# Layer 0 of a two-layer transformer kernel: a PSUM bank of its own for the transposed mixed values, four score banks instead of five

## The chip, the cores and the metric

The kernel runs on one core of one Trainium2 chip. The metric is the device time of one execution in microseconds (us). Three runs of the kernel before gave 1212.03, 1212.92 and 1213.0 us; their median, 1212.92 us, is the time that the change is measured against.

## The reference, cut to what matters

The network is two pre-norm layers over x of 4 sequences x 512 tokens x 256 channels: attention, a routed feed-forward, a second attention, a gated feed-forward, each added to x. The change lies in the first attention (16 heads of 16 channels, causal, 512 tokens):

```python
qkv = jnp.einsum('bsd,od->bso', layernorm(x), w_project)      # q, k, v: 16 heads of 16
att = jnp.einsum('bhqd,bhkd->bhqk', q, k) / math.sqrt(16)
att = jnp.where(causal, -1e9, att)
att = softmax(att)
out = jnp.einsum('bhqk,bhkd->bhqd', att, v)                   # the mixed values
x = x + jnp.einsum('bsd,od->bso', out, w_out)
```

The routed feed-forward that follows in the same layer (router logits for 8 experts per output channel, the two best weighted, 8 expert products) is computed in the kernel at the same time as this attention, in pieces.

## The kernel before, in words

**Blocks and batches.** The 512 positions are cut into four blocks j of 128; block j attends to the keys of blocks 0 to j. A batch n is a block, one of the four sequences s, and a few of the four head groups g (four heads each): 4, 2, 1, 1 groups for j = 0, 1, 2, 3, so 4 + 8 + 16 + 16 = 44 batches (L595 to L600). A batch is treated in five steps:

- `greatest(n)` (L606): the scores with queries as rows, four matmuls per group (one per head, on four row tiles of 32 of TensorE), each head into a PSUM tile of its own of one bank (tag `sc`, L610).
- `mask(n)` (L621): adds the causal mask by matmuls with an identity, then DVE takes the row maxima, one reduction per head (L634).
- `shift(n)` (L639): transposes the maxima on TensorE into the pool `l0_mm` (tag `mm`, one bank), and DVE subtracts them from a row of the queries (L650).
- `powers(n)` (L654): the scores again, with keys as rows, into four more `sc` tiles (L658, matmuls at L664, head the innermost loop); ScalarE takes the exponentials, one instruction per head (L673); GpSimd zeroes the masked corner (L683).
- `mixed(n)` (L691): the product with the values, into the one bank of `l0_mm`, copied out to SBUF by ScalarE (L708).

When the four head groups of a block and sequence are done, `divided(j, s)` (L712) follows in pieces: four transposes of the mixed values into the tile `av_T` (L716, L718); DVE reads its column of sums, L724, and divides, L725, which ends the life of `av_T`; two more transposes `oq_T` (L731, L733), copied out at L736; after the fourth sequence the output products `o` (L742, L745), added to x by DVE (L754).

**Order.** The loop at L776 emits, for each n: `greatest(n+1)`, `shift(n)`, `mask(n+1)`, a `fill`, `mixed(n-1)`, `powers(n)`, another `fill`. A `fill` (L112) gives out work of the streams (generators) as long as a budget for TensorE and DVE lasts: the normalisation and projections of the next block (`prepare`, L561: tiles `x_ps`, `qk_ps`, `v_ps`), `divided`, and the feed-forward (`xT_ps`, `fold`, `lg_ps`, `eo`). The budgets and conditions count slots and made pieces, not PSUM. The instructions of TensorE, DVE and GpSimd keep this program order (`manual_schedule`, L63); in this layer the order of ScalarE and of the DMA queues is left to the framework, which also puts in all waits and gives each tile a bank of its pool when one is free.

**PSUM.** The eight banks: pool `dn`, two (L93; its tiles are `x_ps`, `qk_ps`, `v_ps`, `av_T`, `oq_T`, `o`, `xT_ps`, `fold`, `lg_ps`, `eo`, and it lives through the whole kernel); pool `l0_sc`, five (L437); pool `l0_mm`, one (L438). The last two are given back after layer 0, and the second attention takes those six banks.

The functions that the change touches:

Of the kernel before, what the change touches and what calls it, by code (L numbers as in the profile page):

```python
# [8 lines left out]
F32 = mybir.dt.float32  # L9
# [5 lines left out]
PSUM = bass.MemoryType.PSUM  # L15

P = 128
# [7 lines left out]
NH0 = 16  # L25
# [7 lines left out]
def tile_transformer(  # L33
# [62 lines left out]
    dn = ctx.enter_context(ExitStack())  # L96
    ps_dn = dn.enter_context(tc.tile_pool(name="dn", bufs=2, space=PSUM))
# [13 lines left out]
    def need(engine, cost, gap=0, cond=None):  # L111
        return engine, cost, gap, cond  # L112
# [143 lines left out]
    def hidden_pieces(b):  # L256

        out = []
        done = (4 * b - 5, 1)
        last = b == NBLK - 1  # L260
        yield from norm_pieces(b, b1, b2, out, cond=lambda: b < 2 or done in halves)
        xT = b2.tile([P, 2, 512], F32, tag="xT", name=f"xT{b}")
        for hc in range(2):
            yield need("PE", 0.5, 0 if hc else 1 + last)
            ps = transposed(out[0], hc, ps_dn, "dn", f"xT_ps{b}_{hc}")
            ps = ps.rearrange("p t q -> p (t q)")
            if hc:
                nc.scalar.activation(xT[:, hc, :], ps, AF.Identity, bias=last_16)
            else:
                nc.scalar.copy(xT[:, hc, :], ps)  # L270
        normed.clear()
        xTs[b] = xT
# [159 lines left out]
    with ExitStack() as l0:  # L432
# [1 line left out]
        a1 = l0.enter_context(tc.tile_pool(name="l0_1", bufs=1))  # L434
        a2 = l0.enter_context(tc.tile_pool(name="l0_2", bufs=2))
        a3 = l0.enter_context(tc.tile_pool(name="l0_3", bufs=3))
        ps_sc = l0.enter_context(tc.tile_pool(name="l0_sc", bufs=5, space=PSUM))  # L437
        ps_mm = l0.enter_context(tc.tile_pool(name="l0_mm", bufs=1, space=PSUM))  # L438

        wp = w0.tile([P, 2, 768], F32, name="wp")  # L440
        for hc in range(2):
# [270 lines left out]
        def divided(j, s):  # L712

            yield need("PE", 0.5, 1)
            avs = avs_of.pop((j, s))
            ps = ps_dn.tile([P, NH0, 32], F32, tag="dn", name=f"av_T{j}_{s}")  # L716
            for g in range(4):
                nc.tensor.transpose(  # L718
                    ps[:, 4 * g : 4 * g + 4].rearrange("p h d -> p (h d)"), avs[:, g], ident
                )  # L720
            rden = a2.tile([P, NH0], F32, tag="rden", name=f"rden_{j}_{s}")
            oq = a1.tile([P, NH0, 16], F32, tag="oq", name=f"oq_{j}_{s}")
            yield need("DVE", 0.7, 1)
            nc.vector.reciprocal(rden, ps[:, :, 16])  # L724
            nc.vector.tensor_tensor(  # L725
                oq, ps[:, :, 0:16], rden.unsqueeze(2).to_broadcast([P, NH0, 16]), ALU.mult
            )
            yield need("PE", 0.3, 1)
            if not s:
                aTs[j] = a1.tile([P, 2, 16, NS, 8], F32, tag="aT", name=f"aT{j}")  # L730
            ps = ps_dn.tile([P, 2, P], F32, tag="dn", name=f"oq_T{j}_{s}")  # L731
            for k in range(2):
                nc.tensor.transpose(  # L733
                    ps[:, k], oq[:, 8 * k : 8 * k + 8].rearrange("p h d -> p (h d)"), ident
                )
            nc.scalar.copy(aTs[j][:, :, :, s, :], ps.rearrange("p k (g b) -> p k g b", b=8))  # L736
            if s < NS - 1:
                return

            for t in (0, 2):  # L740
                yield need("PE", 1.75, 1)
                ps = ps_dn.tile([P, 2, HID], F32, tag="dn", name=f"o0_{j}_{t}")  # L742
                for i in range(2):
                    for k in range(2):
                        nc.tensor.matmul(  # L745
                            ps[:, i],
                            lhsT=aTs[j][:, k, 4 * (t + i) : 4 * (t + i) + 4].rearrange(
                                "p g s b -> p (g s b)"
                            ),
                            rhs=wo[:, k, :], start=k == 0, stop=k == 1,  # L750
                        )
                yield need("DVE", 0.7, 1)
                both = xres[:, 4 * j + t : 4 * j + t + 2, :]
                nc.vector.tensor_tensor(both, both, ps, ALU.add)  # L754
            fold_at = streams.index(fold) if fold in streams else len(streams) - 4
            streams.insert(fold_at, Stream(hidden_pieces(j)))


        ps = ps_mm.tile([P, 4, P], F32, tag="mm", name="idle")
# [16 lines left out]
        for n in range(NBT):  # L776
            j, s, gs = batches[n]
# [18 lines left out]
            if n and batches[n - 1][2][-1] == 3:  # L796
                streams.insert(0, Stream(divided(*batches[n - 1][:2])))
# [10 lines left out]
        mixed(NBT - 1)  # L808
        streams.insert(0, Stream(norm_pieces(0, b1, b2, normed_first)))
        last = Stream(divided(*batches[NBT - 1][:2]))  # L810
        streams.insert(0, last)
        while last.next is not None:
# [54 lines left out]
    with ExitStack() as l1:  # L867
# [199 lines left out]
        for p in range(-1, NP):  # L1067
            j, kv = divmod(p, NKV)
# [186 lines left out]
```

## Time and profile before

| | |
|---|---|
| three runs, us | 1212.03, 1212.92, 1213.0 |
| the profiled execution, us | 1213.42 |
| its span in the trace, first to last instruction, us | 1211.7 |
| TensorE busy (PE) | 1168.9 us, 7278 instructions |
| DVE busy | 802.6 us, 1780 instructions |
| ScalarE busy (ACT) | 485.5 us, 1101 instructions |
| layer 0 in the trace | up to about 426 us |
| `av_T`: transposes, reciprocals, divisions | 64, 16, 16 |
| score tiles in `l0_sc` | 176 of `greatest`, 176 of `powers` |

The profile is of one execution. The busy times are the sums of the recorded instructions of an engine; a matmul that has been handed to TensorE and still waits for a bank counts as busy in part, so a busy PE is not PE at work. In the lists, `out<-in` are the program's tile names, `xN` the number of instructions, and a bracket at the end of a line is the idle time of that engine before it and who ended it. PEld is the weight load of TensorE, which overlaps the matmuls.

### The profile page before, as it was taken

How to read it: one execution, taken by the hardware profiler on the slowest of the kernel's cores; microseconds unless marked ns; L12 is line 12 of the kernel's file. 1: busy time of each engine (PE TensorE's matmuls, PEld its weight loads, DVE VectorE, ACT ScalarE, POOL GpSimd, SP SyncE). 2: the span in 40 equal slices, each digit the busy share in tenths (PEclk: the TensorE clock that was granted, in tenths of full speed). 3: DMA queues.
4: the chain of work that ended last, by engine and by line, in shares of the span. 5: the costliest groups of instructions: out<-in, count | busy, mean ns of one | idle time of the engine just before them, and what ended most of it. 6: DMA issues, size and time to landing. Idle time of an engine off the chain costs nothing.

```text
span 1211.7 us, 18780 instructions
## 1 busy us (share of the span) xinstructions
PE 1168.9 (96%) x7278; PEld 679.8 (56%) x7278; DVE 802.6 (66%) x1780; ACT 485.5 (40%) x1101; POOL 121.1 (10%) x155
## 2 busy tenths in 40 slices
PE   6979999999999898999999999999999999999998
PEld 3656555555555543555555555656645456475487
DVE  2555589898887848737886395798499853735710
ACT  1233455664555444434444345355344321312300
POOL 8333321121111000000000000000000000000000
PEclk9899999999999998999999999999999999999999
DMA  7122102000000040000000001021020000000000
GB/s 221 17 56 54 19 4 34 2 1 1 2 1 2 27 147 1 1 1 1 1 1 1 1 1 36 10 55 43 1 62 9 1 1 17 1 1 18 0 1 35
DMA packets 21305, 26.78 MB, mean 22 GB/s; under 512 B 5120, under 2 KB 14592, under 8 KB 21216
## 3 DMA queue, kind: packets, MB, share of 16 engines
q1 hardware_dynamic: 20544, 24.40, 7.6%
q10 hardware_dynamic: 672, 1.18, 0.4%
q8 instruction: 57, 0.93, 0.3%
q14 instruction: 32, 0.26, 0.1%
HBM read 19.27 MB, written 2.10 MB: 18 GB/s over the span
## 4 chain that ended last, share of the span: by engine, by line
PE 81%; DVE 12%; ACT 2%; DMA 2%; issue 1%; SPq 1%; POOL 0%; ACTq 0%; DVEq 0%; POOLq 0%
PE qk_ps L928 10%; PE o L1019 9%; PE y L1175 9%; PE g L856 8%; PE u L856 8%; PE eo L226 8%; PE lg_ps L226 7%; PE s L614 4%; DVE mx L634 3%; PE s L664 3%; PE av L700 2%; PE v_ps L910 2%; PE qk_ps L529 2%; PE s L941 1%; PE a L999 1%
## 5 line engine op out<-in xcount | busy, mean ns | idle before, releaser
L928 PE MATMUL qk_ps<-xT,wqkv 128*128 128x512 f32 x320 | 148.7, 599 | 0.6 <-ACT qT L932 0.6
L226 PE MATMUL lg_ps<-rw,xT 128*128 128x512 f32 x256 | 123.8, 607 | 3.7 <-ACT xT L895 1.7
L226 PE MATMUL eo<-ew,xT 128*128 128x512 f32 x256 | 122.0, 600 | 1.3 <-ACT part L315 1.0
L1019 PE MATMUL o<-wpj,oT 128*128 128x256 f32 x512 | 119.8, 382 | 0.0
L634 DVE TENSOR_REDUCE mx<-s 128x1 f32<-128x384 f32 (+3 forms) x176 | 100.5, 634 | 20.3 <-PE s L629 20.3
L1175 PE MATMUL y<-wd,it 128*128 128x256 f32 x512 | 111.8, 379 | 0.0
L1019 PEld LDWEIGHTS o<-wpj,oT 128*128 128x128 f32 x512 | 95.9, 190 | 28.1 <-issue 15.1
L1175 PEld LDWEIGHTS y<-wd,it 128*128 128x128 f32 x512 | 97.1, 190 | 14.9 <-issue 2.2
L928 PEld LDWEIGHTS qk_ps<-xT,wqkv 128*128 128x128 f32 x320 | 59.3, 190 | 70.0 <-issue 60.2
L673 ACT ACTIVATE pt<-s 128x512 f32<-128x512 f32 (+1 forms) x176 | 83.7, 561 | 34.4 <-PE s L664 34.3
L856 PE MATMUL g<-xT,wgu 128*128 128x512 f32 x192 | 90.4, 593 | 0.0
L856 PE MATMUL u<-xT,wgu 128*128 128x512 f32 x192 | 90.2, 592 | 0.0
L315 ACT ACTIVATE part<-eo,c 128x256 f32<-128x256 f32 x128 | 53.7, 473 | 81.5 <-PE eo L226 76.9
L683 POOL TENSOR_SCALAR_AFFINE_SELECT pt<-pt 128x256 f32<-128x256 f32 (+2 forms) x88 | 55.2, 632 | 268.6 <-ACT pt L673 268.1
L1153 ACT ACTIVATE th<-sq 128x512 f32<-128x512 f32 x64 | 40.3, 629 | 87.6 <-DVE sq L1152 87.6
L177 POOL TENSOR_TENSOR ln_rs<-rs_v,minus_half 128x4 f32<-128x4 f32 x16 | 18.0, 1127 | 563.3 <-DVE rs_v L176 457.9
L226 PEld LDWEIGHTS lg_ps<-rw,xT 128*128 128x128 f32 x256 | 46.5, 192 | 49.0 <-issue 36.9
L226 PEld LDWEIGHTS eo<-ew,xT 128*128 128x128 f32 x256 | 46.4, 190 | 45.8 <-issue 37.0
L614 PE MATMUL s<-qk 32*128 32x128 f32 (+3 forms) x512 | 69.7, 478 | 1.3 <-DMA qk<-stage 0.5
L214 DVE TENSOR_TENSOR xres<-xres,y 128x256 f32<-128x256 f32 x16 | 6.7, 421 | 92.2 <-PE y L1175 92.2
L650 DVE TENSOR_TENSOR qk<-qk,mxT 128x128 f32<-128x128 f32 (+2 forms) x44 | 15.2, 346 | 77.0 <-PE mxT L645 69.3
L289 ACT COPY lg<-lg_ps 128x512 f32<-128x512 f32 x64 | 37.6, 587 | 64.5 <-PE lg_ps L226 64.3
(233 smaller groups left out, 1831.2 us busy)
## 6 DMA issues: line engine op xcount, KB each, us to landing
qk<-stage SPq DMA_DIRECT2D x56, 64.0 KB, 2.4
wqkv<-in_w_qkv SPq DMA_DIRECT2D x8, 320.0 KB, 6.0
rw<-in_router_w SPq DMA_DIRECT2D x8, 256.0 KB, 4.8
ew<-in_expert_w SPq DMA_DIRECT2D x8, 256.0 KB, 5.0
wpj<-in_w_proj SPq DMA_DIRECT2D x1, 2048.0 KB, 11.9
out<-xres SPq DMA_DIRECT2D x4, 512.0 KB, 2.6
xres<-in_x SPq DMA_DIRECT2D x3, 512.0 KB, 8.1
dq_wgu<-in_gate_w SPq DMA_DIRECT2D x8, 128.0 KB, 2.4
```

The costliest lines, as they stand in the source:

```text
L226: nc.tensor.matmul(ps, lhsT=xT[:, hc, (g % 4) * P : (g % 4 + 1) * P], rhs=w[:, hc, 2 * pair : 2 * pair + 2, :].rearrange("p e o -> p (e o) ...
L289: nc.scalar.copy(lg[:, 2 * pair : 2 * pair + 2, :].rearrange("p e o -> p (e o)"), ps)
L315: nc.scalar.mul(part[:, e % 4], ps[:, i], c[:, e : e + 1])
L614: nc.tensor.matmul(tiles[h][:, b * nk : (b + 1) * nk].rearrange("p (c k) -> p c k", k=P), lhsT=queries(j, g)[r, s], rhs=qk[r, g, : j + 1, ...
L634: nc.vector.tensor_reduce(maxes[n % 2][:, :nb, h, 0], ps[:, : nb * nk].rearrange("p (b k) -> p b k", b=nb), AX.X, ALU.max,)
L673: nc.scalar.activation(pt[:, i, : nb * nk], tiles[2 * pair + i][:, : nb * nk], AF.Exp, scale=0.25)
L683: nc.gpsimd.affine_select(out=last, in_=last, compare_op=ALU.is_ge, fill=0.0, base=0, pattern=pattern, channel_multiplier=-1,)
L856: nc.tensor.matmul(ps, lhsT=wgu[:, w, half, jj, par * P : (par + 1) * P], rhs=xT[:, half, :], start=half == 0, stop=half == 1,)
L928: nc.tensor.matmul(ps, lhsT=wqkv[:, hc, kv, h, :], rhs=xT[:, hc, :], start=hc == 0, stop=hc == 1,)
L1019: nc.tensor.matmul(ys[t // 2][:, t % 2], lhsT=state["o"][:, h, t * P : (t + 1) * P], rhs=wpj[:, HPK * kv + h, :], start=kv == 0 and h == 0 ...
L1153: nc.scalar.activation(th, sq, AF.Tanh, scale=0.7978845608028654)
L1175: nc.tensor.matmul(ps, lhsT=it[:, c // 2, c % 2, t * P : (t + 1) * P], rhs=wd[:, c // 2, c % 2, :], start=c == 0, stop=c == 2 * NJ - 1,)
```

## The change

The scores get four banks in place of five, and a new pool of one bank, `l0_t`, holds `av_T`, which was a tile of `dn`. Nothing else is changed: the number of banks, the instructions and the program order of TensorE, DVE and GpSimd stay as they are.

```diff
-        ps_sc = l0.enter_context(tc.tile_pool(name="l0_sc", bufs=5, space=PSUM))
+        ps_sc = l0.enter_context(tc.tile_pool(name="l0_sc", bufs=4, space=PSUM))
         ps_mm = l0.enter_context(tc.tile_pool(name="l0_mm", bufs=1, space=PSUM))
+        ps_t = l0.enter_context(tc.tile_pool(name="l0_t", bufs=1, space=PSUM))
...
             yield need("PE", 0.5, 1)
             avs = avs_of.pop((j, s))
-            ps = ps_dn.tile([P, NH0, 32], F32, tag="dn", name=f"av_T{j}_{s}")
+            ps = ps_t.tile([P, NH0, 32], F32, tag="t", name=f"av_T{j}_{s}")
```

## The prediction, on record before the changed kernel was run

> **What bounds the kernel now.** I read the page first: busy times, then the chain of work that ended last.
>
> ```profile
> PE 1168.9 (96%) x7278; PEld 679.8 (56%) x7278; DVE 802.6 (66%) x1780; ACT 485.5 (40%) x1101; POOL 121.1 (10%) x155
> ...
> PE 81%; DVE 12%; ACT 2%; DMA 2%; issue 1%; SPq 1%; POOL 0%; ACTq 0%; DVEq 0%; POOLq 0%
> ```
>
> TensorE carries 81% of the chain, DVE 12%. PE works in a fixed order, and from 406 to 451.9 us the chain is PE but for a few short copies on ACT (from 424.3 PE alone), so what PE loses or gains by the end of layer 0 reaches the end of the kernel. Then the waits of PE from 45 to 135 us, the stretch where it idles most (line waiting <- who ended it: us, times, longest):
>
> ```profile
> PE qk_ps L529 <- ACT aT L736: 2.0, 2, 1.7
> PE x_ps L202 <- DVE rw L250: 1.3, 1, 1.3
> PE fold L244 <- DVE oq L725: 1.3, 1, 1.3
> PE fold L244 <- ACT xT L268: 0.8, 1, 0.8
> PE qk_ps L529 <- ACT stage L533: 0.7, 1, 0.7
> PE v_ps L551 <- ACT va L557: 0.7, 1, 0.7
> ```
>
> These are tiles of dn that wait for the reader of the dn tile just before them: qk_ps at 51.60 for the copy of the qk_ps before it, although dn has two banks. The other bank is held by av_T, from its transposes (48.55) to the end of L725 (59.02). All sixteen av_T live so, 1.5 to 11 us each. While one lives, dn is a single bank.
>
> The timeline shows the score banks (start, length):
>
> ```profile
> 340.44 1.14 PE L614 MATMUL s<-qk 32*128 32x512 f32 x8
> ...
> 346.02 2.07 ACT L673 ACTIVATE pt<-s 128x512 f32<-128x512 f32 x4 [0.85 <-PE s L664]
> 346.46 2.31 PE L614 MATMUL s<-qk 32*128 32x512 f32 x8
> 347.16 0.29 PEld L614 LDWEIGHTS s<-qk 32*128 32x128 f32 x2 [0.20 <-ACT pt L673]
> 347.65 0.29 PEld L614 LDWEIGHTS s<-qk 32*128 32x128 f32 x2 [0.20 <-ACT pt L673]
> ...
> 311.75 1.17 PE L664 MATMUL s<-qk 32*128 32x128 f32 x32
> ...
> 318.08 2.48 DVE L634 TENSOR_REDUCE mx<-s 128x1 f32<-128x512 f32 x4
> 319.23 1.94 PE L664 MATMUL s<-qk 32*128 32x128 f32 x32
> 320.01 0.96 PEld L664 LDWEIGHTS s<-qk 32*128 32x128 f32 x26 [0.30 <-DVE mx L634]
> ```
>
> greatest takes 1.14 us when its banks are free, 2.31 when the exponentials of the powers before it have just begun: its heads then start 0.49 us apart, as the exponentials end. powers takes 1.17 us free, 1.94 when it follows the reductions closely. By the start of each weight load, head h waits for the reader of head h-1 of the group before: with five banks and four tiles per group the rotation is one ahead. These stalls are inside matmul groups that count as busy.
>
> [...] the trace grants 0.50 in two slices of 3.4 us from 86.2 to 93.0, 0.53 in the next and 1.00 after it.
>
> **The change, part 1: av_T leaves dn.** No instruction is added, and PE, DVE and POOL keep their order. Every other dn tile then waits for the tile two before it, never later than now. I walk PE's shift through the trace (minus is earlier). A wait of x idle us is worth x + 0.16, since a queued matmul otherwise starts 0.16 before the recorded end of the one ahead.
> - 46.8 to 67.1: powers +0.60 (part 2), then qk_ps at 51.60 -0.84, v_ps at 58.63 -0.83, qk_ps at 67.13 -1.81 (idle 0.68, 0.67, 1.65): -2.9.
> - 72.7 to 84.0: powers twice +0.60; av_T and oq_T at 74.67 and 75.86 get -1.0. None of this counts: greatest at 76.20 waits for the DMA of qk, which follows the qk_ps of 67.13, and oq_T at 84.03 waits 1.81 for DVE, which is 2.8 early. -2.8.
> - 84.9 to 93.6: the first x_ps, at 89.46, waited for L250 to free fold's bank; its data (xn) ended at 88.12, now 85.3: it starts at 85.35, -4.1. The second waits for fold's reader, now done by 86.5, not for ACT: 86.55 for 91.22, -4.7. fold at 93.01 no longer waits for ACT: -5.3.
> - The clock in that stretch: at half rate av L700 takes 1.94 for 1.08, powers 1.54 for 1.17, two x_ps 1.1 each for 0.61, in all 2.2 us lost. [...] The trace can't show how much: nothing to 1.7, I take 0.8: -6.1.
> - 114.67: fold waited 1.30 for L725. It starts 1.46 earlier, but the v_ps after it then waits for L754 to free o's bank (116.5 for 117.37): -0.8 is kept.
> - 129.3 to 132.5: xT_ps, fold and lg_ps idle 0.68, 0.78, 0.16; lg_ps still needs the copy L268, which ends at 131.25 for 131.9 after: 131.3 for 132.54, -1.2.
> - Later av_T: two waits (0.34 at 252.91, 0.40 at 283.08), eaten by the next greatest, which waits for exponentials. Nothing.
> With +0.16 for one greatest, the sum at 148 us is **-8.0**; ends -6 (no clock gain, the copies on ACT in a worse order) and -10.
>
> **Part 2: four score banks.** Head h now waits for the reader of head h itself, so a group that is stalled ends one reader later: 0.49 us (exponential of 512 columns), 0.38 (384), 0.60 or 0.46 (reduction of 512 or 384). For each of the 42 greatest and 43 powers that follow a group I took the end of the last reader + 0.05 (its end to the next weight load, 347.11 to 347.16) less the start of head 3's load:
>
> | block | greatest later: times, us | powers later: times, us |
> |---|---|---|
> | 0 | 1, 0.5 | 3, 2.0 |
> | 1 | 3, 0.6 | 1, 0.6 |
> | 2 | 6, 1.8 | 5, 1.4 |
> | 3 | 13, 5.8 | 7, 3.3 |
>
> Blocks 0 and 1 are in the walk above. Blocks 2 and 3 sum to 12.3 us, not all of it on the path. greatest's stall stays where DVE idled for it: L650 then starts later and takes the delay on (idle 2.2 us before L650 at 282.50, 2.1 at 317.87, 2.9 at 367.19). powers' stall is mostly lost behind DVE: the next exponentials stand on ACT behind L406 or L383, which wait for a DVE chain (at 305, 364, 390 us) that the late powers hasn't moved. Walking PE's and DVE's shift side by side: block 2 +1.3 by 226, greatest at 250.45 +0.4 (DVE sets the rest there), greatest and powers at 269 to 290 +0.7, to 341 another +1.9 (greatest at 297, 305, 315, 323, 331, 340, mostly in the order of 0.3 to 0.5, some of it covered), then +0.49 each at 363.7, 373.1 and 389.4, +0.5 for powers at 395.28, which PE's next L650 takes on: **+6.3**. Ends +4.5 and +12.3 (nothing absorbed). What is queued behind a stalled greatest: the transposed maxima, L650, the reductions, and the product in the next fill.
>
> **Sum.** -8.0 + 6.3 = -1.7 us. The profiled execution took 1213.42 (span 1211.7 and 1.7 around it), so it would take 1211.7; it lay 0.5 above the median of the runs. Against that median: 1212.92 - 1.7 = **1211.2 us**.
>
> **Rivals.**
> - The losses are absorbed more, and the clock doesn't drop at 86 us: -9.7 + 4.8 = -4.9, **1208.0**. For: DVE is 82 to 96% busy in blocks 2 and 3, with long stretches that set PE's pace. Against: in block 3 the greatest that stall are mostly those DVE waits for.
> - Slower: the fourth bank is the bottleneck in block 3 and nothing is absorbed, +12.3 - 8.0 = +4.3, **1217.2**. For: 13 of block 3's 16 greatest are late by the new count. It decides from a loss of 8.0, two thirds of the 12.3. Against: the DVE chains at 305, 364 and 390.
> - The change does nothing that counts: early gains are lost to DVE's long stretch from 148 to 168 us, and the stalls too, **1212.9**. Against: DVE idled before L650 at 148.07 and so starts that stretch earlier.
> One unknown is in all: ACT's order, which the framework chooses anew. Other copies ahead of the exponentials cost up to 0.6 each; I give it 1.5 us both ways.
>
> **How the numbers follow.** About 0.2%, 2.4 us, is what a measurement can tell from none. Forecast: 0.55, from 1209 to 1213.5, of which 0.2 lies below 1210.5. First rival 0.24, second 0.16, third 0.05. Faster by over 0.2%: 0.2 + 0.24 = 0.44. Slower: 0.16. Same: 0.40. The range takes in the first rival and most of the way to the second: 1207.5 to 1216.
>
> **What would show it.** After: PE's waits for L533, L557, L250 and L725 from 45 to 135 us gone or halved, and 148 us' L650 some 8 us earlier; half clock after 86 us shorter. greatest when stalled 0.4 to 0.5 us longer (2.8 for 2.31), its first load waiting for ACT too; powers 2.5 for 1.94; layer 0's end at 426 us 1 to 3 us earlier. I am wrong if the L650 of 148 us moves by less than 5 us, or if greatest and powers lose over 8 us after it.

## The result, and the profile after

The changed kernel took 1217.57 us (median of 6 runs, 1216.99 to 1220.25) against 1212.09 for the kernel before beside it: ratio 1.0046, interval 1.0033 to 1.0059. It is slower by about 5.5 us. The prediction said 1211.2, with a range up to 1216.0. The profiled execution took 1216.99 us, with a span of 1215.3 against 1211.7.

The busy times of the changed kernel:

```profile
PE 1177.2 (97%) x7277; PEld 688.0 (57%) x7278; DVE 801.7 (66%) x1780; ACT 484.6 (40%) x1101; POOL 120.9 (10%) x155
```

TensorE is "busy" for 8.3 us more with the same instructions (one record is missing): they last longer, where a matmul waits inside its record for a bank (the `greatest` of batch 38 takes 2.59 us for 2.31) or where the granted clock is 0.50 (four matmuls of one `qk_ps` take 3.06 us for 1.99). The other engines do what they did.

**Where it came from.** All lines after the diff's first hunk are one further in the changed kernel (L650 is L651). I follow one instruction, the subtraction L650 of `shift`, which every batch has, and count its place from the first `x_ps` (13.41 us before, 12.48 after), so that the start of the execution drops out. Up to the L650 of 148.07 us the changed kernel gains 4.3 us; from there to the last L650 (400.83) it loses 8.3; after that the two traces keep their distance to within 0.5 us. The prediction had -8.0 and +6.3. So the gain was half of what I took, and the loss a third more. Both of the prediction's own signs of being wrong came: less than 5 us at the L650 of 148 us, more than 8 lost after it.

PE's waits of the changed kernel from 45 to 135 us (line waiting <- who ended it: us, times, longest):

```profile
PE av_T L719 <- DVE oq L726: 1.9, 1, 1.9
PE qk_ps L530 <- ACT stage L534: 1.9, 1, 1.9
PE av L701 <- DVE qk L651: 0.4, 2, 0.2
...
PE qk_ps L530 <- DVE rw L250: 0.3, 1, 0.3
```

The waits that I wanted gone are gone (v_ps for L557, x_ps for L250, fold for L725). Two of 1.9 us stand: one of `qk_ps`, which I had counted as won, and a new one of `av_T` itself. Here is the first. The timeline of the kernel before (start, length, and in brackets the idle time before and its releaser):

```profile
64.11 0.59 ACT L533 COPY stage<-qk_ps 128x512 f32<-128x512 f32 x1
64.75 2.06 ACT L673 ACTIVATE pt<-s 128x512 f32<-128x512 f32 x4
```

The timeline of the changed kernel, the same two and the `qk_ps` that follows:

```profile
62.85 2.06 ACT L674 ACTIVATE pt<-s 128x512 f32<-128x512 f32 x4 [0.53 <-PE s L665]
...
64.78 0.62 ACT L534 COPY stage<-qk_ps 128x512 f32<-128x512 f32 x1
...
65.45 3.06 PE L530 MATMUL qk_ps<-xT,wp 128*128 128x512 f32 x4 [1.87 <-ACT stage L534]
```

Before, the copy of the `qk_ps` of 60.46 us stood ahead of the four exponentials; in the changed kernel the framework put it behind them, though its data were ready at 60.4. Of the `dn` tiles in between, `fold` and `oq_T`, the second took the bank of the first; the `qk_ps` at 65.45 needs the one that this copy frees, and waits 1.87 us, longer than the 1.65 before. Its four matmuls also take 3.06 us for 1.99: the granted clock was 0.50 from 66.2 to 69.6.

The late half shows as predicted. `greatest` of batch 38, changed kernel (346.46 us before):

```profile
347.53 2.06 ACT L674 ACTIVATE pt<-s 128x512 f32<-128x512 f32 x4 [0.85 <-PE s L665]
...
348.18 0.29 PEld L615 LDWEIGHTS s<-qk 32*128 32x128 f32 x2 [0.38 <-ACT pt L674]
348.18 2.59 PE L615 MATMUL s<-qk 32*128 32x512 f32 x8
348.67 0.29 PEld L615 LDWEIGHTS s<-qk 32*128 32x128 f32 x2 [0.20 <-ACT pt L674]
```

All four heads now start as exponentials end, the first too. The group lasts 2.59 us for 2.31 and begins later: the wait of its first head has left the group and stands ahead of it. Counted from the start of the exponentials, the group ends 3.24 us later, against 2.75 before: the 0.49 of one exponential that was forecast. That is why the summed length of `greatest` in block 3 is not longer than before (31.0 us against 32.9); the loss shows in PE's and DVE's waits from 148 to 430 us instead. First DVE of the kernel before (L629 is a mask matmul of PE, which the profile names as the releaser of two of these waits):

```profile
DVE qk L650 <- PE mxT L645: 27.3, 17, 3.2
DVE qk L650 <- PE s L629: 7.7, 2, 5.0
```

DVE of the changed kernel:

```profile
DVE qk L651 <- PE mxT L646: 38.7, 17, 3.7
```

The 5.0 of the kernel before is the wait ahead of the L650 of 148.07 us itself; in the changed kernel that one ends at 142.8 and isn't in the list. Like with like, DVE waited 30.0 us before and 38.7 after: 8.7 more, about the late loss of 8.3.

PE of the changed kernel, from 135 us (the kernel before has no such wait there):

```profile
PE s L615 <- ACT pt L674: 3.0, 5, 0.9
```

And a thing that the prediction priced only as a small gain: the granted clock. From 148 us to the last L650 the kernel before ran 3.4 us at half rate (granted clock 0.50), the changed one 13.7. Busy times by stretch in the changed kernel, 3.41 us on each side of the step of its clock at 161.79 (length, then PE, PEld, DVE, ACT and POOL with their counts, the granted clock, the DMA share and GB/s):

```profile
158.38:161.79 3.41, 2.38 (x46) 1.84 (x47) 3.38 (x9) 1.34 (x4) 0.00 (x0) 1.00 0.00 0
161.79:165.20 3.41, 3.24 (x24) 2.29 (x19) 2.48 (x6) 2.41 (x6) 1.73 (x2) 0.50 0.00 0
```

### The profile page after: what moved, and what is told of

It is laid out like the page before. It is cut to its first block, busy times and chain, and to the rows that moved or that the text cites. A ratio compares the mean times of both kernels' runs of the same rounds, so it can differ in the third digit from the quotient of the medians.

```text
span 1215.3 us, 18782 instructions
## 1 busy us (share of the span) xinstructions
PE 1177.2 (97%) x7277; PEld 688.0 (57%) x7278; DVE 801.7 (66%) x1780; ACT 484.6 (40%) x1101; POOL 120.9 (10%) x155
## 4 chain that ended last, share of the span: by engine, by line
PE 83%; DVE 11%; ACT 3%; DMA 1%; issue 1%; SPq 0%; POOL 0%; ACTq 0%; DVEq 0%; POOLq 0%
PE qk_ps L929 10%; PE o L1020 9%; PE y L1176 9%; PE g L857 8%; PE u L857 8%; PE eo L226 8%; PE lg_ps L226 8%; PE s L615 5%; DVE mx L635 3%; PE s L665 3%; PE v_ps L911 2%; PE qk_ps L530 2%; PE av L701 2%; PE s L942 1%; PE a L1000 1%
## 5 line engine op out<-in xcount | busy, mean ns | idle before, releaser
L226 PEld LDWEIGHTS lg_ps<-rw,xT 128*128 128x128 f32 x256 | 46.8, 194 | 48.3 <-issue 37.5
L651 DVE TENSOR_TENSOR qk<-qk,mxT 128x128 f32<-128x128 f32 (+2 forms) x44 | 15.2, 344 | 84.4 <-PE mxT L646 84.3
```

Source lines behind the costliest of these rows:

```text
L226: nc.tensor.matmul(ps, lhsT=xT[:, hc, (g % 4) * P : (g % 4 + 1) * P], rhs=w[:, hc, 2 * pair : 2 * pair + 2, :].rearrange("p e o -> p (e o) ...
```

## The experiments

The theory that I went into them with: the mechanism of part 2 is right at its price, part 1 was cut short by ACT's order and by the wait of `av_T` for its own bank, and the clock did the rest. The rivals: the early gain can't last whatever the banks; or the loss isn't the fourth bank's but the clock's. All but e3, e8 and after_again use one score pool of five named banks and pick them by hand; the computation stays whole in all, and only e9 adds to it. Each ratio is against the kernel before on the same chip. In the table, "early" is the change against before from the first `x_ps` to the L650 of 148 us, "late" from there to the last L650, "half" the time at half rate in the late part, all from each kernel's one trace.

| kernel | early, us | late, us | half, us | median, us | ratio (interval) |
|---|---|---|---|---|---|
| before | 0 | 0 | 3.4 | see text | 1 |
| changed, first / again | -4.3 / -3.8 | +8.3 / +8.3 | 13.7 / 13.7 | 1217.57 / 1217.96 | 1.0046 / 1.0045 (1.0033 to 1.0058) |
| e1_switch | -2.8 | +0.4 | 3.4 | 1211.43 | 0.998 (0.9971 to 0.9989) |
| e2_late4 | +1.8 | +7.9 | 13.7 | 1222.32 | 1.0066 (1.0042 to 1.0091) |
| e3_four_only | +2.3 | +9.3 | 10.2 | 1225.22 | 1.0089 (1.007 to 1.0109) |
| e4_s3_in_dn | -0.4 | +2.1 | 10.2 | 1214.33 | 1.0009 (0.9998 to 1.002) |
| e5_copy_first | -7.1 | +3.6 | 17.1 | 1209.25 | 0.9972 (0.9963 to 0.9981) |
| e6_divide_at_once | -3.9 | +2.3 | 13.7 | 1210.71 | 0.9977 (0.9968 to 0.9986) |
| e7_greatest_spared | -4.1 | +2.9 | 6.8 | 1211.62 | 0.9996 (0.9988 to 1.0004) |
| e8_after_copy_first | -6.2 | +13.0 | 20.5 | 1215.56 | 1.0021 (1.0009 to 1.0033) |
| e9_warm | -6.4 | +1.3 | 6.8 | 1207.38 | 0.9946 (0.9924 to 0.9967) |
| e10_five_first | -8.2 | +0.4 | 3.4 | 1205.75 | 0.9935 (0.9914 to 0.9957) |

The kernel before had medians of 1213.26, 1212.33 and 1212.35 in the three groups (e1 to e4; again, e5 to e7; e8 to e10), each measured on a chip of its own; between groups the ratios are the safer measure.

**e1_switch: the change only where it helps.** Where the first argument of `score_tiles` is true, the score tiles take the five banks in turn; where it is false, banks 0 to 3, and `av_T` has bank 4. The edit against the changed kernel, in part:

```diff
...
+            k = turn[0]
+            turn[0] = k + 4 if five else 0
...
+                    [P, 512], F32, tag=f"sc{(k + h) % 5 if five else h}", name=f"{name}_{h}"
...
-            tiles = [ps_sc.tile([P, 512], F32, tag="sc", name=f"s1_{n}_{h}") for h in range(4)]
+            tiles = score_tiles(n > 14, f"s1_{n}")
...
-            tiles = [ps_sc.tile([P, 512], F32, tag="sc", name=f"s2_{n}_{h}") for h in range(4)]
+            tiles = score_tiles(n > 13, f"s2_{n}")
...
-            ps = ps_t.tile([P, NH0, 32], F32, tag="t", name=f"av_T{j}_{s}")
+            if j < 2:
+                ps = ps_sc.tile([P, NH0, 32], F32, tag="sc4", name=f"av_T{j}_{s}")
+            else:
+                ps = ps_dn.tile([P, NH0, 32], F32, tag="dn", name=f"av_T{j}_{s}")
```

> Four score banks and av_T in the fifth only for blocks 0 and 1 (up to batch 14, about 150 us); from there five score banks, and av_T back in dn. Theory (the early gain is real and the loss is made after 148 us by the fourth bank): L650 of 148 us comes some 4.9 us earlier than before, as in the changed kernel, nothing is given back after it, about 1207.2 against 1212.1. Rival (what is gained early is lost anyway in DVE's long stretches and to half-rate clock after 148 us, whatever the banks): 1210.5 to 1212.5.

Measured: 1211.43, 1.8 to 2.4 us below before. The late part is +0.4: nothing is given back in this trace once five banks are there, so the rival's reason, that DVE takes the gain anyway, falls. But the time missed the theory's 1207.2 and lies in the rival's range: the early gain in this trace was only 2.8, and 13 of the 22 runs had a mean clock of 0.982, where the trace had 0.986, so the rival's other reason, the clock, isn't excluded.

**e2_late4: the complement.** The two conditions are turned round (`n < 15`, `n < 14`, `j > 1`).

> The complement: five score banks with av_T in dn for blocks 0 and 1, the changed allocation only from batch 14 on. Theory: nothing moves up to 150 us; after it the stalls cost about the 6.3 of the prediction, 1218.4; 8.2, 1220.3, if the half-rate clock at 161.8 us comes without the early part too. Rival (the loss is mostly clock and the early part's disturbance of ACT's order, not the fourth bank): 1213 to 1215.

Measured: 1222.32, 8 us above before by the ratio, 9 in the medians; late +7.9. That is above the theory's 1220.3 too. The loss is made by the late part alone, and the rival of 1213 to 1215 falls. Naming the banks by hand moves nothing by itself: up to batch 9 the L650 stay within 0.8 us of before. Up to 148 us this kernel has the banks of before, and yet its trace is 1.8 behind: it ran 17.1 us at half rate between 84 and 136 us, the trace of before 10.2. So two traces with the same banks lie 1.8 us apart there, the one behind with 6.9 us more at half rate.

**e3_four_only: part 2 alone.** Pool `l0_sc` of four, `av_T` in `dn`, the eighth bank unused.

> Four score banks throughout, av_T left in dn, the eighth bank unused: part 2 alone. Theory: the early stalls of blocks 0 and 1 (at most 3.7 us, some absorbed) add to the 6.3 to 8.2 of blocks 2 and 3: 1219.5 to 1223. Rival (the stalls are absorbed by DVE's stretches and the changed kernel lost time in the own bank of av_T): 1213 to 1216.

Measured: 1225.22, 11 to 12 us above before, early +2.3 and late +9.3: some 2 us above the theory's range and far from the rival's, so the theory was right in kind and too low. The gain of part 1 is thus worth some 5 us in the changed kernel by the ratios (1.0089 to 1.0046).

**e4_s3_in_dn: one `av_T` taken out of its own bank.** The condition of e1 becomes `j < 2 and (j, s) != (0, 3)`.

> As e1_switch, but av_T of block 0, sequence 3, which waited 1.9 us in the changed kernel for the division of sequence 2 to leave the one bank, stands in dn. Theory (this wait is a step that the prediction left out): the oq_T after it starts about 1.4 us earlier and 1 to 2 us of it reach the end, 1205.5 to 1206.5. Rival (the x_ps after it waits for the normalisation anyway): the same as e1_switch within 0.5 us.

Both missed: it is 2.9 us slower than e1_switch in the median. PE's waits of e4 from 80 to 125 us:

```profile
PE x_ps L202 <- DVE rw L250: 1.4, 1, 1.4
PE oq_T L747 <- DVE oq L739: 1.2, 1, 1.2
PE x_ps L202 <- ACT xT L582: 0.7, 1, 0.7
PE fold L244 <- ACT xT L582: 0.7, 1, 0.7
```

These are the waits of the kernel before. This one `av_T`, out of `dn`, is most of part 1's gain (L650 of batches 4 to 8: -4.2 in e1, -0.8 here); what its own wait costs can't be seen this way.

**after_again: the changed kernel once more.**

> The changed kernel once more, as the measure for the other three on this chip: 3 to 6 us above the kernel before, by how often the clock drops in each; in the trace, L650 of 148 us some 5 us earlier and layer 0's end some 3 later than before, counted from the first x_ps.

1217.96; the trace repeats the first (-3.8, +8.3, and 6.8 us at half rate from 163).

**e5_copy_first: ACT's order.** e1_switch, with one copy moved ahead:

```diff
-            nc.scalar.copy(stage[:, i], ps)
+            with tc.high_priority(offset=AHEAD if (j, half, i) == (1, 1, 0) else 0):
+                nc.scalar.copy(stage[:, i], ps)
```

> As e1_switch, but the copy of one qk_ps (block 1, second half, first tile) has priority on ACT and lands behind the first exponential of sequence 2, not behind the fourth. Theory (the order on ACT kept the wait of the qk_ps of 67 us at 1.9 us): that wait falls to about 0.4, the next greatest starts 1.5 us earlier, and 1 to 2.5 us of it, with the half-rate window at 66 to 69 us gone, reach 148 us; the whole 1 to 2.5 below e1_switch. Rival (the oq_T copy or the exponentials pushed back by 0.6 us take it): equal to e1_switch within 0.5.

Timeline of e5:

```profile
63.09 0.60 ACT L685 ACTIVATE pt<-s 128x512 f32<-128x512 f32 x1 [0.53 <-PE s L676]
...
63.59 0.58 ACT L545 COPY stage<-qk_ps 128x512 f32<-128x512 f32 x1
64.05 1.60 ACT L685 ACTIVATE pt<-s 128x512 f32<-128x512 f32 x3
64.22 1.98 PE L540 MATMUL qk_ps<-xT,wp 128*128 128x512 f32 x4 [0.40 <-ACT stage L545]
```

The wait fell from 1.87 to 0.40 and the half rate behind it went. From batch 2 to batch 4 the trace gains 1.7 us on before, where e1 and the changed kernel lost 1.3 to 1.4. Early is -7.1. The whole is 2.2 us below e1_switch in the medians, 1.0 by the ratios: less than the 4.3 by which the early parts differ. Its trace ran 10.2 us at half rate from 158 us, of which e9 tells more. That the order on ACT kept the wait is shown; what the end saw of it went with the mean clock of the run (the times are with e9).

**e6_divide_at_once: the wait of `av_T` for its bank.** e1_switch, with the reciprocal and division of block 0, sequence 2 emitted at once (`if (j, s) != (0, 2)` ahead of the `yield need("DVE", 0.7, 1)`); the `oq_T` and `fold` behind it move up on PE.

> As e1_switch, but the division of block 0, sequence 2 is emitted right behind its transposes, ahead of the normalisation of block 2 on DVE (the oq_T and the fold behind it move up with it). Theory (the one bank of av_T waited 1.9 us for this division): av_T of sequence 3 waits no more, x_ps of 89 us starts 1.4 to 1.9 us earlier and about that much reaches 148 us; 1 to 2 us below e1_switch. Rival (DVE then waits for the transposes, or the normalisation comes late by as much): no gain, or up to 1 us slower than e1_switch.

PE's waits of e6 from 80 to 125 us begin:

```profile
PE x_ps L202 <- DVE xn L186: 1.5, 1, 1.5
```

The wait of `av_T` is gone, but the second half of `x_ps` now waits 1.5 us for its data, and early is -3.9, no better than the changed kernel. The theory falls: taking away the bank wait that I had overlooked gains nothing, because the normalisation on DVE ends no sooner. The median, 0.7 below e1's, is less than the 1.8 us between the two early parts with the same banks (e2).

**e7_greatest_spared: which stall counts.** From batch 14 on the score tiles have fixed banks, 4, 0, 1, 2 for `greatest` and 0 to 3 for `powers`:

```diff
-            k = turn[0]
-            turn[0] = k + 4 if five else 0
+            k = 4 if five and name[1] == "1" else 0
```

> As e1_switch up to batch 14; after it the score tiles have fixed banks: powers the banks 0 to 3, greatest the banks 4, 0, 1, 2. So greatest waits as with five banks and powers as with four (its third tile waits for the last reduction). Theory (powers' stall is mostly lost behind DVE, greatest's is what counts): 0.5 to 1.5 us above e1_switch after 150 us. Rival (the two count alike, by their raw sums 4.7 for powers and 7.6 for greatest in blocks 2 and 3): 2.5 to 4.7 us above it.

In the trace `powers` of block 3 is as long as in the changed kernel (24.1 us in all, 23.7 there, 21.4 before), while behind the half rate of 161 to 168 us the late part adds 0.8. So a stall of `powers` is lost behind DVE, as the prediction said, and the loss is `greatest`'s. The median is 0.2 us above e1's, though by the ratios it is 1.9 (they were measured in different groups); 2.5 to 4.7 is excluded by the trace, and the times can't part 0.5 from 1.9.

**e8_after_copy_first: the changed kernel with ACT's order mended.** The edit of e5 in the changed kernel.

> The changed kernel with only the copy of e5_copy_first moved ahead on ACT. Theory (the prediction's early part was right but for ACT's order): from the first x_ps to L650 of 148 us the gain is about 7 us, against 4.3 in the changed kernel and 8.0 in the prediction; after it the four banks cost 6.5 to 8.3 as before. So about 2.8 below the changed kernel, 1214.5 to 1215.5. Rival (the early gain is lost to the later stalls, or the other order costs elsewhere): within 1 us of the changed kernel, 1217 to 1218.5.

1215.56, 2.4 us below the changed kernel, early -6.2: the theory held but for a few tenths, the rival not. Its trace was its slowest execution (1219.46, 20.5 us at half rate), so its late part isn't compared.

**e9_warm: the clock.** e5 with matmuls that feed nothing, where PE waits at 156 us for DVE to have read the one bank of `l0_mm`:

```diff
+            if n == 13:
+                ps = ps_dn.tile([P, 512], F32, tag="dn", name="warm")
+                for i in range(3):
+                    nc.tensor.matmul(
+                        ps, lhsT=ident, rhs=wp[:, 0, :512], start=not i, stop=i == 2,
+                    )
             with tc.high_priority(offset=AHEAD):
```

> As e5_copy_first, with three matmuls 128x512 added whose result nobody reads, ahead of the product of batch 12 at 156 us, where TensorE waits 1.2 us for DVE. Theory (this pause and the sparse powers behind it make the clock halve from 158 to 168 us): no half rate there, 2 to 3 us below e5_copy_first where that had it, 1206 to 1207.5. Rival (the pause isn't what decides, or the matmuls outlast it): half rate as in e5_copy_first, equal or up to 0.5 us slower.

The same stretch in e5, then in e9 (columns as above):

```profile
158.00:161.40 3.40, 3.40 (x26) 2.76 (x26) 3.30 (x8) 1.73 (x5) 0.72 (x1) 0.50 0.00 0
161.40:164.80 3.40, 3.23 (x17) 1.70 (x17) 0.02 (x1) 1.27 (x3) 0.56 (x2) 0.50 0.00 0
164.80:168.20 3.40, 3.40 (x12) 2.77 (x10) 3.37 (x12) 0.51 (x2) 0.00 (x0) 0.50 0.00 0
```

```profile
158.00:161.40 3.40, 3.40 (x56) 2.10 (x54) 3.37 (x11) 0.85 (x3) 0.00 (x0) 1.00 0.00 0
161.40:164.80 3.40, 2.38 (x20) 1.44 (x20) 1.32 (x3) 2.39 (x6) 1.31 (x2) 1.00 0.00 0
164.80:168.20 3.40, 3.40 (x13) 1.96 (x12) 3.37 (x12) 0.51 (x2) 0.00 (x0) 1.00 0.00 0
```

The added matmuls take 2.79 us, more than the 1.2 of the wait; without the half rate the stretch from batch 11 to 16 is still 2.5 us shorter than in e5, and the median is 1.9 lower (3.1 by the ratios). All six runs had a mean clock of 0.986 or 0.987, eight of e5's ten 0.983 (1209.06 to 1209.58); e5's other two, at 0.987 and 0.989, took 1207.24 and 1207.13, as long as e9's. So what was gained goes with the clock. With the pause filled the clock stayed up in these runs; but e10, without the added matmuls, has the same pause (1.21 us at 155.99) and no half rate behind it, so the pause alone doesn't decide.

**e10_five_first.** e5, with the fifth bank also for `powers` of batch 0, 11 us before `av_T` first needs it (banks 0,1,2,3 and 4,0,1,2 for `greatest` 0 and 1, 3,4,0,1 for `powers` 0, then 2,3,0,1).

> As e5_copy_first, but powers of batch 0 has the fifth score bank too, which av_T doesn't need yet (it takes it at 48 us). Theory (the prediction's walk left out the two stalls before 46 us, 0.8 and 0.5 us): powers of batch 0 ends 0.6 to 0.8 us earlier and TensorE reaches the x_ps of 45 us that much earlier; the whole 0.5 us faster, less than the runs can tell. Rival: DVE sets that stretch (L650 of 45 us waits for it), no difference at 55 us.

1205.75, the fastest of all: 6.6 us below before in the medians, 7.9 by the ratio, and 12 below the changed kernel. The L650 of batch 0 lies 0.3 us ahead of the kernel before; in the ten traces with four score banks there it lies 0.2 to 0.6 behind. By the L650 of batch 2 (55.32 us before) e10 is 1.0 ahead of e5, which had 6.8 us at half rate in between where e10 had 3.4, and 0.7 ahead of the first trace of the changed kernel, which had 3.4 as well: the rival falls. Early is **-8.2** and late +0.4. That it gains 3.5 us over e5 where its edit explains under 1 goes for the most part with the clock: its trace has 3.4 us at half rate in the late part, e5's 17.1, and four of its six runs had a mean clock of 0.987 to 0.990. DVE's wait for the transposed maxima from 148 to 430 us is back at its old value, 30.8 us against 30.0.

## Why the prediction was wrong, step by step

- **The bound and the banks: right.** PE's loss and gain in layer 0 reach the end. The other `dn` tiles lose their waits once `av_T` has left, and the stalls of `greatest` end one reader later, the first head waiting too.
- **Part 1, -8.0: the step that failed.** The walk counted -1.81 for `qk_ps` at 67.13, on the rule that a `dn` tile "waits for the tile two before it, never later than now". With `oq_T` in the free bank, it waited for the third before it, the `qk_ps` of 60.46, whose copy had been done early in the order that ACT had before; the framework chose another, with four exponentials first. I had put that risk at "1.5 us both ways" and outside the sum. It cost 3.1 us on the spot: between the L650 of batch 2 and of batch 4 every kernel with this copy behind the exponentials lost 1.3 to 1.4 (changed, e1, e4, e6, e7), and every one with the copy moved gained 1.7 (e5, e8, e9, e10), against about -2.6 in the walk. 1.5 of it is the wait, 1.1 the `qk_ps` behind it at half rate (3.06 us for 1.98), the rest what follows; in the whole kernel it is 2.0 to 2.4 us (e8 against the two medians of the changed kernel). The half rate at 66 to 69 us stood in the traces of all those with the late copy and in none with it moved; but the kernel before, with a wait of 1.65, kept the clock there.
- **Two stalls left out of the walk.** The table had 0.8 and 0.5 us in block 0 before 46 us, "in the walk above", but the walk began at 46.8. Lending the fifth bank to `greatest` 1 and `powers` 0 got 0.7 to 1.0 us back (e10), and the early part then measured -8.2.
- **`av_T` waiting for its own bank: overlooked, and nothing to be gained by removing it** (e6). Moving it back into `dn` is what costs (e4).
- **The rest of the walk: right.** For 84.9 to 93.6 us the walk goes from -2.8 to -6.1, so -3.3; from batch 4 to batch 6 the changed kernel gained 3.6. For 114.67 and 129.3 to 132.5 it has -0.8 and -1.2; from batch 7 to 8 and from 9 to 10 the L650 gained 0.8 and 1.2. So the whole of part 1's error was made before batch 4.
- **Part 2, +6.3: right in mechanism, and about in size.** At 10 to 14 us of half rate the late part of kernels with five banks for `greatest` is +2.1 and +2.3 (e4, e6), with four +7.9 to +9.3 (changed, e2, e3): a difference of about 6 to 7. Counted from the L650 of batch 14, behind the half rate of 161 to 168 us, the changed kernel loses 6.6, e1 and e10 0.1.
- **The clock: the term that was missing from the loss.** I priced half rate only as a gain of 0.8 at 86 us, an estimate (the traces have 10.2 us of half rate there before, 6.8 in the changed kernel). In the late part it cost the changed kernel 1.4 in the trace (batch 12 to 14, +1.74 against +0.34 in e1, whose trace had none there). The prediction's sum had nothing for it there. In the medians it is more. Of the 100 runs of before in the three groups, 67 had a mean clock of 0.987 or above (mean 1211.9 us) and 22 one of 0.981 to 0.984 (1215.5); of 11 runs of the changed kernel none was above 0.985, and nine lay at 0.982 or 0.983 (1218.0). At a like clock the change costs 2.5 us; the other 3 of the 5.5 go with the clock, which is no longer found at its higher values. That is a comparison of runs, not a trial: no run here held the clock, and what keeps it down in the changed kernel isn't shown. In the traces, the way from -1.7 to +4.0 (-4.3 and +8.3) is 3.7 from part 1, 1.4 from this clock and 0.6 from the rest of the late part.
- **The rivals.** The slower one named 1217.2, near the time, but by another sum: all 12.3 us of stalls on the path against a full gain. The stalls were absorbed to about half, as forecast; the gain was halved and the mean clock was lower (0.982 or 0.983 in nine of 11 runs). So the reason wasn't that one. The other two, 1208.0 and 1212.9, fall with the time.

In the traces of the kernel before and the changed one half rate came in stretches of 3.41 us, or of two or three times that (86.0 to 96.2 us before, 161.8 to 168.6 changed), and the same banks up to 148 us gave 10.2 us of it between 84 and 136 us in one trace and 17.1 in another: its amount isn't set by the banks alone. In e9, with one pause of 1.2 us filled, a wait for the one bank of `l0_mm`, 10.2 us of half rate were gone; that e10 kept the clock with the same pause shows that such a pause isn't enough.

**What stays open.** Why the framework put the copy behind the exponentials was not tried. What sets the granted clock wasn't shown: in the 3.41 us before 161.79 us TensorE in the changed kernel was busy for 2.38 by the records, and the clock went to 0.50; in the 3.41 us from 161.06 on in the kernel before it was busy for 1.94, and the clock stayed at 1.00. Nor do the busy times settle it: records of matmuls that wait for a bank count as busy.

## What to carry to other kernels

When an edit gives a tile another bank, the wait can move to that bank's last reader (here the copy at 64.78 us, a wait of 1.87), so look up where this reader stands in its engine's queue, and if a scheduler places it, price the case that it lands behind everything ready by then. A bank can be lent by phase instead of given for good: here it is worth up to 8 us before 148 us, with ACT's order mended, and 6 to 7 to the scores after it. Giving it had a ratio of 1.0046, lending it 0.998 (e1), and lending it with the copy moved and the first batches served too 0.9935 (e10). Where an edit moves the waits of TensorE, allow for another granted clock too (here 13.7 us at half rate in the late part for 3.4), and compare runs at a like mean clock before a difference of 3 us is explained by waits.

## What the runs showed of the hardware that was not expected

The mean granted clock of a run takes a few values (six in the 100 runs of before, 0.979 to 0.989) and goes with its time: 8 runs of before at 0.979 averaged 1217.4 us, 22 at 0.981 to 0.984 1215.5, 67 at 0.987 or above 1211.9. That is more than the whole effect of many edits, in a kernel whose instructions are the same. Three matmuls whose result nobody reads, 2.79 us of TensorE, went with a kernel 1.9 us faster in the medians, 3.1 by the ratios; it is as fast as the kernel without them in the two of ten runs that had the higher clock.
